# Two of the seven Strassen products split once more into 128x128 blocks, with the masks on GpSimd, the norm in one ScalarE operation and a new order of the steps

## The chip, the cores and the metric

The kernel runs on one core of a Trainium2 chip. The metric is the device time of one execution in microseconds (us), median of several. A ratio is the mean time of one kernel's fast runs over the mean of the fast runs of the kernel before in the same rounds, so it is not quite the ratio of the medians beside it. Spans and positions inside a group come from one profiled execution each; "wait" is the time by which TensorE's matmuls start further apart than their usual pitch, averaged over the 28 inner groups of four batches. In the profiles PE is TensorE's matmuls and PEld its weight loads, DVE VectorE, ACT ScalarE, POOL GpSimd and SPq the queue of SyncE, which issues DMAs.

## The reference, cut to what matters

```python
h = relu(layernorm(x))                                   # x: 128 batches x 128 nodes x 512
A = einsum('od,bdn->bon', adj, h); C = A + b             # same matrix twice, so (C - A) is the bias
x = x + max over nodes of relu(A + b)
h = relu(layernorm_of_the_new_x)
q, k, v = h @ Wq + bq, h @ Wk + bk, h @ Wv + bv          # 512 x 512, 8 heads of 64
w = softmax(q k^T / 8 + (-1e9 where adj == 0))
out = x + w v
```

The first layer adds one number to each row of x, which the layer norm of the second removes again. So the kernel norms x once. Nearly all arithmetic is in the three 512x512 projections, in f32.

## The kernel before: the parts that the argument touches

Batches go in groups of four. A projection of a group is a product of 512x512 by 512x512, done by Strassen's algorithm (Winograd's form) on 256x256 quarters: seven products P1 to P7 in place of eight. A product is eight matmul instructions of 256 columns (four f32 matmuls in two instructions each). VectorE (DVE) adds up the products, because each PSUM bank holds a running sum that several results share.

```python
class Products:                       # one projection ("q", "k" or "v") of a group; cut
    def p1(self):
        self.a = self.bank(0);  self.mm(self.a, "a11", "b11", True)
        ...                           # ScalarE copies bank a out, with two biases: p1a, p1b
    def p6(self):
        self.b = self.bank(1);  self.mm(self.b, "s2", "t2", True)
        nc.vector.tensor_tensor(self.u2, self.b, self.pf[0], op=ALU.add)
    def p2(self):
        self.mm(self.a, "a12", "b21");  self.biased(self.dst(0, 0), self.a, 0)
    def p7(self):
        self.mm(self.b, "s3", "t3")
        nc.vector.tensor_tensor(self.u3, self.b, self.pf[1], op=ALU.add)
    def p5(self):
        self.c = self.bank(2);  self.mm(self.c, "s1", "t1", True)
        self.add(self.dst(1, 1), self.c, self.u3)
    def p4(self):
        self.mm(self.b, "a22", "t4");  self.add(self.dst(1, 0), self.b, self.pf[1])
    def p3(self):
        self.mm(self.c, "s4", "b22");  self.add(self.dst(0, 1), self.c, self.u2)
...
part = (v.p1, v.p6, v.p2, v.p7, v.p5, v.p4, q.p1, v.p3, q.p6, q.p2, q.p7, q.p5,
        q.p4, k.p1, q.p3, k.p6, k.p2, k.p7, k.p5, k.p4, k.p3)      # TensorE's order in a group
```

Each group begins with `apply` (w v of the group before) and `scores` (q k^T), then come the projections. The masks multiply w by 0 where adj is 0. Between those steps stands the work for the group after next: `norm` (the layer norm), `adjacency` (the product with adj), `blocks` (a DVE transpose in 32x32 blocks) and `move`, which brings the blocks of a pair of batches into their places, 16 DMAs for each pair on SyncE's queue. `h_sum` makes the quarter sums t1 to t4 from what has landed.

## Time and profile before

| | |
|---|---|
| median | 1546.77 us (1546.75 to 1548.46) |
| period of a group, start of apply to start of apply | 47.55 us |
| first apply starts / last apply to the end | 88.9 / 13.0 us |
| waits in TensorE's stream, per group | about 0.5 us, all at the three changes of matmul kind (k to apply, apply to scores, scores to v); the same in the changed kernel |

The page says how busy each engine was, and the chain which work ended last; the prediction shows both.

The columns are start, duration, engine, line, operation and count.

### The profile page before, as it was taken

The numbers are of one execution on the slowest core, as the hardware profiler recorded it, in microseconds if no ns is written. First come the engines' busy times: TensorE is split into PE (matmuls) and PEld (weight loads), VectorE is DVE, ScalarE is ACT, GpSimd is POOL, SyncE is SP. The second block draws the span as 40 slices with busy tenths as digits, with TensorE's granted clock in tenths as the row PEclk, the third lists the DMA queues.
The fourth block names the chain that finished last, engine by engine and source line by source line (L and its number), as shares of the span: only waits on it lengthen the run. The fifth ranks groups of instructions, "written<-read, shape, count | busy, mean of one in ns | idle before, by whom it ended". The sixth has DMA issues, their size and how long they took to land.

```text
span 1544.7 us, 29809 instructions
## 1 busy us (share of the span) xinstructions
PE 1528.1 (99%) x11805; PEld 1310.5 (85%) x11805; DVE 1129.9 (73%) x2115; ACT 415.2 (27%) x844; POOL 272.4 (18%) x278
## 2 busy tenths in 40 slices
PE   7999999999999999999999999999999999999997
PEld 6888888888888888888888888888888888888886
DVE  7677777777777777777777777777777777777756
ACT  3322223222232222332222322223222133222221
POOL 5411122111221111220112211122111122011200
PEclk9999999999999999999999999999999999999999
DMA  5223322123221232222332212322123221233101
GB/s 180 35 72 80 78 59 72 49 75 83 56 74 48 72 83 55 78 49 71 80 75 60 72 49 76 83 55 74 49 72 83 55 77 47 72 80 74 36 30 56
DMA packets 307789, 105.10 MB, mean 68 GB/s; under 512 B 273152, under 2 KB 273280, under 8 KB 307648
## 3 DMA queue, kind: packets, MB, share of 16 engines
q1 hardware_dynamic: 306352, 101.00, 25.3%
q8 instruction: 95, 1.56, 0.4%
q10 hardware_dynamic: 1120, 1.90, 0.4%
q14 instruction: 46, 0.38, 0.1%
q0 software_dynamic: 176, 0.27, 0.1%
HBM read 37.03 MB, written 33.55 MB: 46 GB/s over the span
## 4 chain that ended last, share of the span: by engine, by line
PE 98%; DMA 1%; DVE 0%; ACTq 0%; ACT 0%; POOL 0%; DVEq 0%; issue 0%
PE bk L387 75%; PE bk L512 8%; PE bk L482 8%; PE bk L321 7%; PE bk L458 1%; DMA xg<-in_x_dram 1%; DVE o L530 0%; ACTq L237 0%; DVE o L540 0%; DVE live L552 0%; ACT hn L283 0%; POOL rstd L275 0%; DVE st L270 0%; PE bk L315 0%; DVE RS L529 0%; DVEq L668 0%
## 5 line engine op out<-in xcount | busy, mean ns | idle before, releaser
L275 POOL TENSOR_TENSOR rstd<-ve,mhalf 128x1 f32<-128x1 f32 x128 | 83.6, 653 | 1039.6 <-DVE ve L273 1023.5
L490 ACT ACTIVATE w<-bk 128x512 f32<-128x512 f32 x256 | 128.8, 625 | 401.6 <-PE bk L482 401.6
L289 POOL TENSOR_TENSOR xg<-xg,bv_sb 128x512 f32<-128x512 f32 x128 | 173.6, 1357 | 140.6 <-DVE hn L280 140.6
L494 DVE TENSOR_TENSOR w<-w,live 128x512 f32<-128x512 f32 x256 | 184.4, 731 | 0.4 <-ACT w L490 0.4
L387 PE MATMUL bk<-hs,sk_sb 128*128 128x256 f32 x768 | 181.1, 379 | 0.0
L387 PE MATMUL bk<-sv_sb,hs 128*128 128x256 f32 x768 | 176.2, 379 | 0.0
L387 PE MATMUL bk<-hs,sq_sb 128*128 128x256 f32 x744 | 175.6, 379 | 0.0
L387 PEld LDWEIGHTS bk<-hs,sk_sb 128*128 128x128 f32 x768 | 145.9, 190 | 33.5 <-issue 7.9
L283 ACT ACTIVATE hn<-hn,rstd 128x512 f32<-128x512 f32 x128 | 92.5, 723 | 283.8 <-DVE hn L280 257.0
L387 PEld LDWEIGHTS bk<-hs,sq_sb 128*128 128x128 f32 x744 | 141.4, 190 | 32.0 <-issue 7.2
L387 PEld LDWEIGHTS bk<-sv_sb,hs 128*128 128x128 f32 x768 | 145.9, 190 | 19.8
L426 DVE TENSOR_TENSOR u<-bk,p1a 128x512 f32<-128x512 f32 x95 | 65.7, 692 | 125.9 <-PE bk L387 125.9
L321 PE MATMUL bk<-hn,adjT 128*128 128x512 f32 x256 | 131.4, 596 | 0.0
L512 PEld LDWEIGHTS bk<-v,w 128*64 128x64 f32 x4096 | 122.1, 137 | 10.6 <-issue 10.6
L512 PE MATMUL bk<-v,w 128*64 128x65 f32 x4096 | 126.5, 222 | 0.0
L387 PE MATMUL bk<-wv_sb,hT 128*128 128x256 f32 x512 | 124.3, 386 | 0.0
L482 PE MATMUL bk<-qT,kT 64*128 64x128 f32 x2048 | 122.9, 275 | 0.0
L387 PE MATMUL bk<-hT,wk_sb 128*128 128x256 f32 x512 | 121.0, 379 | 0.0
L482 PEld LDWEIGHTS bk<-qT,kT 64*128 64x128 f32 x2048 | 116.8, 188 | 2.5 <-issue 0.3
L387 PE MATMUL bk<-hT,wq_sb 128*128 128x256 f32 x496 | 117.2, 379 | 0.0
L387 PEld LDWEIGHTS bk<-hT,wq_sb 128*128 128x128 f32 x496 | 94.2, 190 | 25.6 <-issue 14.3
L387 PEld LDWEIGHTS bk<-hT,wk_sb 128*128 128x128 f32 x512 | 97.3, 190 | 13.2
(87 smaller groups left out, 1994.8 us busy)
## 6 DMA issues: line engine op xcount, KB each, us to landing
out_dram<-o SPq DMA_DIRECT2D x128, 256.0 KB, 2.2
xg<-in_x_dram SPq DMA_DIRECT2D x62, 512.0 KB, 4.7
hT<-tb SPq DMA_DIRECT2D x992, 32.0 KB, 1.9
wq_sb<-in_L_gnn_Wq_dram SPq DMA_DIRECT2D x2, 512.0 KB, 6.8
xg<-in_x_dram ACTq DMA_DIRECT2D x3, 256.0 KB, 7.0
wk_sb<-in_L_gnn_Wk_dram SPq DMA_DIRECT2D x1, 512.0 KB, 11.2
wv_sb<-in_L_gnn_Wv_dram SPq DMA_DIRECT2D x1, 512.0 KB, 12.2
wk_sb<-in_L_gnn_Wk_dram ACTq DMA_DIRECT2D x1, 512.0 KB, 9.7
```

The lines of the kernel that those rows point to most:

```text
L275: nc.gpsimd.tensor_tensor(rstd, ve, mhalf, op=ALU.pow)
L283: nc.scalar.activation(HN[m], HN[m], AF.Copy, scale=RSTD[m])
L289: nc.gpsimd.tensor_tensor(x_m, x_m, bv_sb, op=ALU.add)
L321: nc.tensor.matmul(pa, adjT, HN[m], start=True, stop=True)
L387: nc.tensor.matmul(bank[:, r, :], lhs, rhs, start=first and r == 0 and c == 0, stop=r == 1 and c == 1, skip_group_check=True,)
L426: nc.vector.tensor_tensor(self.u2, self.b, self.pf[0], op=ALU.add)
L458: nc.tensor.matmul(pq[:, r, :], W["q"][:, c, (2 * f + r) * P : (2 * f + r + 1) * P], h[:, :, c], start=r == 0 and c == 0, stop=r == 1 and ...
L482: nc.tensor.matmul(psc[j][:, f, :], KT[g][r, f, i * D : (i + 1) * D], QT[g][r, f, i * D : (i + 1) * D], start=True, stop=True,)
L490: nc.scalar.activation(w[:, j], psc[j], AF.Exp, scale=HD ** -0.5)
L494: nc.vector.tensor_tensor(w[:, j], w[:, j], live_h, op=ALU.mult)
L512: nc.tensor.matmul(pav[r, c : c + HE], w[:, h % 2, h // 2, r], V[:, i, h, :], start=True, stop=True,)
```

## The change

It has three intents. P4 and P3 are split by the same algorithm into 128x128 blocks: seven block products M1 to M7 for each of the two, so 14 f32 matmuls of 128 columns in place of eight of 256. To give DVE room for the extra additions, the masks go to GpSimd and the norm becomes one ScalarE operation. And as the blocks need a scratch bank, the banks and the order of the whole group are dealt anew. The core of the diff, cut:

```diff
+            def p43(self):                 # in place of p4 and p3, both at once (k = 0, 1)
+                scr = bank(6).rearrange("p (m k d) -> p m k d", m=2, k=2)
+                def m1(k): mm(scr[:, 0, k], ...)      # M1, M6, M7 one after another in here
+                def m5(k): mm(scr[:, 1, k], ...)      # same bank, other half
+                ...
+                m1(0), m1(1), m5(0), m5(1)
+                more(u[:, :, 0, 0], scr[:, 0])        # DVE: u += M1
+                m2(0), m3(0), m6(0), m6(1)
+                more(u[:, :, 0, 1], scr[:, 0])
+                m4(0), m2(1), m3(1), m4(1), m7(0), m7(1)
+                ...                                   # four more additions of u
+                self.add(self.dst(1, 0), self.b, self.u[:, 0])
+                self.add(self.dst(0, 1), self.c, self.u[:, 1])
...
         def norm_end(m):
-            nc.vector.tensor_scalar(HN[m], X[g][:, i, :], MV[m][:, 0:1], 0.0, op0=ALU.subtract, op1=ALU.max)
-            nc.scalar.activation(HN[m], HN[m], AF.Copy, scale=RSTD[m])
+            nc.scalar.activation(HN[m], x_of(m), AF.Relu, scale=RSTD[m], bias=NMR[m])
...
-            pa = bank(5 + i % 2)
+            pa = bank(7)
...
-                6: [(blocks, m)], 7: [(blocks, m + 1), (move, m + 1)],
-                ...
-                14: [(blocks, m + 3), (move, m + 3)],
-                17: [(adjacency, m + 2)], 19: [(adjacency, m + 3)],
+                6: [(norm, m + 1)], 7: [(norm_end, m + 1)], 8: [(blocks, m), (adjacency, m)],
+                9: [(norm, m + 2)],
+                12: [(blocks, m + 1), (move, m + 1), (norm_end, m + 2), (adjacency, m + 1)],
+                13: [(norm, m + 3)], 14: [(norm_end, m + 3), (adjacency, m + 2), (blocks, m + 2)],
+                15: [(blocks, m + 3), (move, m + 3)], 16: [(adjacency, m + 3)],
...
+                for p in [Products(g, "v")] + [Products(g + 1, n) for n in "qk" if g + 1 < NG]:
+                    part += p.p1, p.p6, p.p2, p.p7, p.p5, p.p43
...
-                    for k, s in enumerate((6, 9, 12, 13, 15, 16, 17, 18)):
-                        add(s, mask, b + k // 2, k % 2)
+                    for k, s in enumerate((9, 10, 11, 12, 13, 14, 15, 16)):
+                        add(s, mask, nc.gpsimd, b + k // 2, k % 2)
```

So there are 18 steps to a group now, six for each projection; steps 6 to 11 are q's, 12 to 17 k's.

More of the change, by code (lines that the diff above doesn't have):

```diff
@@ L188, in tile_adj_preln_d2 @@
     WS = {n: const.tile([P, 4, 2, N // 2], F32, name=f"s{n}_sb") for n in "qkv"}
+    WB = {n: const.tile([P, 2, 4, P], F32, name=f"ss{n}_sb") for n in "qkv"}
     b0_sb = const.tile([P, 1], F32, name="b0_sb")
@@ L202, in fast @@
     def fast(ctx):
-        xpool = ctx.enter_context(tc.tile_pool(name="xpool", bufs=4))
+        xpool = ctx.enter_context(tc.tile_pool(name="xpool", bufs=7))
         proj = ctx.enter_context(tc.tile_pool(name="proj", bufs=2))
@@ L211, in fast, with x_of, load @@
         CNT, w_of, O = [], {}, {}
-        X, HN, TB, HT, HB, QT, KT, C, AMAX, WA, RSTD, MV, PR = ({} for _ in range(13))
+        X, HN, TB, HT, HB, H2, QT, KT, C, AMAX, WA, RSTD, NMR, PR = ({} for _ in range(14))
         def bank(k):
             return ps.tile([P, 512], F32, name=f"bk{k}")
-        def load(g):
-            X[g] = xpool.tile([P, G, N], F32, name="xg")
-            for i in range(0, G, 2):
-                nc.sync.dma_start(
-                    X[g][:, i : i + 2, :],
-                    x[g * G + i : g * G + i + 2].rearrange("b p n -> p b n"),
-                )
+        def x_of(b):
+            return X[b // 2][:, b % 2, :]
+        def load(p):
+            X[p] = xpool.tile([P, 2, N], F32, name="xp")
+            nc.sync.dma_start(X[p], x[2 * p : 2 * p + 2].rearrange("b p n -> p b n"))
         def load_w(eng, name, h):
@@ L234, in fast @@
         nc.scalar.dma_start(adj_sb, adj)
-        X[0] = xpool.tile([P, G, N], F32, name="xg")
+        for p in range(2):
+            X[p] = xpool.tile([P, 2, N], F32, name="xp")
         for i in range(G):
-            (nc.scalar if i > 0 else nc.sync).dma_start(X[0][:, i, :], x[i])
+            (nc.scalar if i > 0 else nc.sync).dma_start(x_of(i), x[i])
         load_w(nc.sync, "q", 0)
@@ L247, in fast @@
         nc.gpsimd.dma_start(bv_sb, bv.rearrange("(o f) -> o f", o=1).to_broadcast([P, N]))
-        load(1)
-        load(2)
+        for p in range(2, 5):
+            load(p)
         make_identity(nc, ident)
@@ L266, in norm @@
                 C[g] = stat.tile([P, G], F32, name="c")
-            HN[m] = work.tile([P, N], F32, name="hn")
+            HN[m] = work.tile([P, N], F32, name="hn", bufs=3)
             st = stat.tile([P, 6], F32, name="st")
             mv = stat.tile([P, 2], F32, name="mv")
-            nc.vector.bn_stats(st, X[g][:, i, :])
+            nc.vector.bn_stats(st, x_of(m))
             nc.vector.bn_aggr(mv, st)
@@ L275, in norm @@
             nc.gpsimd.tensor_tensor(rstd, ve, mhalf, op=ALU.pow)
-            MV[m] = mv
+            nmr = NMR[m] = stat.tile([P, 1], F32, name="nmr")
+            nc.gpsimd.tensor_scalar(nmr, mv[:, 0:1], rstd, -1.0, op0=ALU.mult, op1=ALU.mult)
         def norm_end(m):
-            g, i = divmod(m, G)
-            nc.vector.tensor_scalar(
-                HN[m], X[g][:, i, :], MV[m][:, 0:1], 0.0, op0=ALU.subtract, op1=ALU.max
-            )
-            nc.scalar.activation(HN[m], HN[m], AF.Copy, scale=RSTD[m])
+            nc.scalar.activation(HN[m], x_of(m), AF.Relu, scale=RSTD[m], bias=NMR[m])
             if m >= G:
@@ L287, in add_bv @@
         def add_bv(m):
-            x_m = X[m // G][:, m % G, :]
+            x_m = x_of(m)
             nc.gpsimd.tensor_tensor(x_m, x_m, bv_sb, op=ALU.add)
@@ L339, in h_sum, with h_blocks, weight_blocks @@
             nc.vector.tensor_sub(HB[g][o], HB[g][a], HB[g][b])
+        def h_blocks(g, k):
+            if k == 0:
+                H2[g] = one.tile([P, 2, 4, D], F32, name="h2")
+            b, t = HB[g]["t4 b22".split()[k]].rearrange("p t c d -> p c t d"), H2[g][:, k]
+            nc.vector.tensor_sub(t[:, 0:2], b[:, :, 1], b[:, 0])
+            nc.vector.tensor_sub(t[:, 2], b[:, 1, 1], t[:, 0])
+            nc.vector.tensor_sub(t[:, 3], b[:, 1, 0], t[:, 2])
+        def weight_blocks(eng, n):
+            for k in range(2):
+                a = WA[n]["a22 s4".split()[k]].rearrange("p c (o f) -> p o c f", o=2)
+                s = WB[n][:, k]
+                for o, x, op, y in (
+                    (s[:, 0], a[:, 1, 0], ALU.add, a[:, 1, 1]),
+                    (s[:, 2], s[:, 0], ALU.subtract, a[:, 0, 0]),
+                    (s[:, 1], a[:, 0, 0], ALU.subtract, a[:, 1, 0]),
+                    (s[:, 3], a[:, 0, 1], ALU.subtract, s[:, 2]),
+                ):
+                    eng.tensor_tensor(o, x, y, op=op)
         def weight_sum(eng, n, k):
@@ L363, in __init__ @@
                 self.g, self.n = g, n
+                self.k0 = 3 if n == "q" else 0
                 if n == "q":
@@ L393, in bank @@
             def bank(self, k):
-                return bank(k).rearrange("p (r n) -> p r n", r=2)
+                return bank(self.k0 + k).rearrange("p (r n) -> p r n", r=2)
             def biased(self, out, bank, f):
@@ L412, in p1 @@
                 self.mm(self.a, "a11", "b11", True)
-                self.pf = [tmp.tile([P, 2, HT2], F32, name="p1a")]
+                self.u = tmp.tile([P, 2, 2, HT2], F32, name="u")
                 if self.n == "v":
+                    self.pf = [self.u[:, 0]] * 2
                     nc.scalar.copy(self.pf[0], self.a)
-                    self.pf.append(self.pf[0])
                 else:
-                    self.pf.append(tmp.tile([P, 2, HT2], F32, name="p1b"))
+                    self.pf = [tmp.tile([P, 2, HT2], F32, name="p1a", bufs=1), self.u[:, 0]]
                     for f in range(2):
@@ L424, in p6 @@
                 self.mm(self.b, "s2", "t2", True)
-                self.u2 = tmp.tile([P, 2, HT2], F32, name="u2")
-                nc.vector.tensor_tensor(self.u2, self.b, self.pf[0], op=ALU.add)
+                nc.vector.tensor_tensor(self.u[:, 1], self.b, self.pf[0], op=ALU.add)
             def p2(self):
@@ L440, in p5, with blk, mm, m1 @@
                 self.add(self.dst(1, 1), self.c, self.u3)
+            def p43(self):
+                a = [WA[self.n][k].rearrange("p c (o f) -> p o c f", o=2) for k in ("a22", "s4")]
+                b = [HB[self.g][k].rearrange("p t c d -> p c t d") for k in ("t4", "b22")]
+                s, t = WB[self.n], H2[self.g]
+                scr = bank(6).rearrange("p (m k d) -> p m k d", m=2, k=2)
+                def blk(x):
+                    if self.n == "v":
+                        return x.rearrange("p t (o d) -> p o t d", o=2)
+                    return x.rearrange("p o (t d) -> p o t d", t=2)
+                def mm(out, w, h, start=False):
+                    lhs, rhs = (h, w) if self.n == "v" else (w, h)
+                    nc.tensor.matmul(
+                        out, lhs, rhs, start=start, stop=True, skip_group_check=True
+                    )
+                bc = [blk(self.b), blk(self.c)]
+                u = self.u.rearrange(
+                    "p k t (o d) -> p k o t d" if self.n == "v" else "p k o (t d) -> p k o t d",
+                    d=D,
+                )
+                def m1(k):
+                    mm(scr[:, 0, k], a[k][:, 0, 0], b[k][:, 0, 0], start=k == 0)
+                def m2(k):
+                    mm(bc[k][:, 0, 0], a[k][:, 0, 1], b[k][:, 1, 0])
+                def m3(k):
+                    mm(bc[k][:, 0, 1], s[:, k, 3], b[k][:, 1, 1])
+                def m4(k):
+                    mm(bc[k][:, 1, 0], a[k][:, 1, 1], t[:, k, 3])
+                def m5(k):
+                    mm(scr[:, 1, k], s[:, k, 0], t[:, k, 0])
+                def m6(k):
+                    mm(scr[:, 0, k], s[:, k, 2], t[:, k, 2])
+                def m7(k):
+                    mm(scr[:, 0, k], s[:, k, 1], t[:, k, 1])
+                def more(to, what):
+                    nc.vector.tensor_tensor(to, to, what, op=ALU.add)
+                m1(0), m1(1), m5(0), m5(1)
[3 more added lines that the diff above has]
+                m4(0), m2(1), m3(1), m4(1), m7(0), m7(1)
+                for o in range(2):
+                    more(u[:, :, o, 1], scr[:, 1])
+                for t_ in range(2):
+                    more(u[:, :, 1, t_], scr[:, 0])
+                self.add(self.dst(1, 0), self.b, self.u[:, 0])
+                self.add(self.dst(0, 1), self.c, self.u[:, 1])
@@ L447, in p3 @@
                 self.mm(self.c, "s4", "b22")
-                self.add(self.dst(0, 1), self.c, self.u2)
+                self.add(self.dst(0, 1), self.c, self.u[:, 1])
         def plain_q(t, f):
@@ L490, in scores, with mask @@
                     nc.scalar.activation(w[:, j], psc[j], AF.Exp, scale=HD ** -0.5)
-        def mask(b, j):
+        def mask(eng, b, j):
             w = w_of[b]
-            nc.vector.tensor_tensor(w[:, j], w[:, j], live_h, op=ALU.mult)
+            eng.tensor_tensor(w[:, j], w[:, j], live_h, op=ALU.mult)
         def apply(g, n_last=G):
@@ L537, in residual @@
             y = O[g][:, i]
-            x_b, c_b = X[g][:, i, :], C[g][:, i : i + 1]
+            x_b, c_b = x_of(b), C[g][:, i : i + 1]
             if eng is nc.vector:
@@ L559, in next_norms @@
             return {
-                1: [(norm, m)], 2: [(norm_end, m), (norm, m + 1)], 4: [(norm_end, m + 1)],
-                6: [(blocks, m)], 7: [(blocks, m + 1), (move, m + 1)],
-                8: [(adjacency, m)], 9: [(norm, m + 2)],
-                10: [(adjacency, m + 1), (norm_end, m + 2)],
-                11: [(norm, m + 3)], 12: [(norm_end, m + 3)], 13: [(blocks, m + 2)],
-                14: [(blocks, m + 3), (move, m + 3)],
-                17: [(adjacency, m + 2)], 19: [(adjacency, m + 3)],
+                1: [(norm, m)], 2: [(norm_end, m)],
+                6: [(norm, m + 1)], 7: [(norm_end, m + 1)], 8: [(blocks, m), (adjacency, m)],
[3 more added lines that the diff above has]
+                15: [(blocks, m + 3), (move, m + 3)], 16: [(adjacency, m + 3)],
             }
@@ L575, in fast @@
                     transposes(m - 1)
+                if m == 2:
+                    adjacency(0)
             nc.vector.tensor_single_scalar(live, adjT, 0.0, op=ALU.not_equal)
-            for m in (2, 3):
-                adjacency(m - 2)
-                transposes(m)
+            transposes(2)
+            adjacency(1)
+            transposes(3)
             adjacency(2)
@@ L607, in fast @@
                     f(m)
+            weight_blocks(nc.gpsimd, "v")
             weight_sums(nc.gpsimd, "q")
+            weight_blocks(nc.gpsimd, "q")
             for m in range(G):
                 add_bv(m)
+            weight_blocks(nc.gpsimd, "k")
             for g in range(NG):
@@ L615, in fast @@
                 scores(g)
-                v = Products(g, "v")
-                if g + 1 < NG:
-                    q, k = [Products(g + 1, n) for n in "qk"]
-                    part = (
-                        v.p1, v.p6, v.p2, v.p7, v.p5, v.p4, q.p1, v.p3, q.p6, q.p2, q.p7, q.p5,
-                        q.p4, k.p1, q.p3, k.p6, k.p2, k.p7, k.p5, k.p4, k.p3,
-                    )
-                else:
-                    part = (v.p1, v.p6, v.p2, v.p7, v.p5, v.p4, v.p3)
+                part = []
+                for p in [Products(g, "v")] + [Products(g + 1, n) for n in "qk" if g + 1 < NG]:
+                    part += p.p1, p.p6, p.p2, p.p7, p.p5, p.p43
                 todo = {s: [] for s in range(len(part))}
@@ L628, in add @@
                     todo[s].append(what)
+                if g == 0:
+                    for k in range(2):
+                        h_blocks(0, k)
                 if g + 1 < NG:
@@ L633, in fast @@
                             residual(b - G + i)
-                    for k in range(4):
-                        add((0, 3, 5, 8)[k] if g > 0 or k == 3 else 3 + k, h_sum, g + 1, k)
+                    for k, s in enumerate((0 if g else 3, 2 if g else 3, 3, 7)):
+                        add(s, h_sum, g + 1, k)
+                    for k, s in enumerate((8, 9)):
+                        add(s, h_blocks, g + 1, k)
                     if g + 2 < NG:
@@ L640, in fast @@
                     else:
-                        add(4, count, 0, b)
-                    for k, s in enumerate((6, 9, 12, 13, 15, 16, 17, 18)):
-                        add(s, mask, b + k // 2, k % 2)
+                        add(6, count, 0, b)
+                    for k, s in enumerate((9, 10, 11, 12, 13, 14, 15, 16)):
+                        add(s, mask, nc.gpsimd, b + k // 2, k % 2)
+                    if g + 2 < NG:
+                        add(0, load, 2 * g + 5)
                     if g + 3 < NG:
-                        add(10, load, g + 3)
+                        add(8, load, 2 * g + 6)
                 else:
-                    for k, s in enumerate((0, 0, 0, 1, 2, 2, 3, 4)):
-                        add(s, mask, b + k // 2, k % 2)
-                    for i, s in enumerate((0, 1, 2, 3)):
+                    for k, s in enumerate((0, 0, 0, 1, 2, 2, 3, 3)):
+                        add(s, mask, nc.vector, b + k // 2, k % 2)
+                    for i, s in enumerate((0, 1, 2, 5)):
                         add(s, residual, b - G + i)
```

## The prediction

> **What bounds the kernel now.** I read the page first, then the chain of waits in order of time, then the timeline of one group of four batches.
>
> ```profile
> PE 1528.1 (99%) x11805; PEld 1310.5 (85%) x11805; DVE 1129.9 (73%) x2115; ACT 415.2 (27%) x844; POOL 272.4 (18%) x278
> ...
> PE 98%; DMA 1%; DVE 0%; ACTq 0%; ACT 0%; POOL 0%; DVEq 0%; issue 0%
> PE bk L387 75%; PE bk L512 8%; PE bk L482 8%; PE bk L321 7%; PE bk L458 1%; DMA xg<-in_x_dram 1%; DVE o L530 0%; ACTq L237 0%; DVE o L540 0%; DVE live L552 0%; ACT hn L283 0%; POOL rstd L275 0%; DVE st L270 0%; PE bk L315 0%; DVE RS L529 0%; DVEq L668 0%
> ```
>
> The chain is TensorE alone, three quarters of it in the projections (L387). It waits for nobody: DVE has 27% spare, ACT and POOL far more. In the merged chain,
>
> ```profile
> 96.57 15.74 PE bk L387 x72
> 117.48 12.09 PE bk L387 x56
> 144.12 15.74 PE bk L387 x72
> ```
>
> 12.09/56 = 0.216 us per matmul instruction of 256 columns (each f32 matmul is two instructions), and 144.12 - 96.57 = 47.55 us is the period of a group. It adds up without a hole: 84 products' matmuls x 2 x 0.216 = 36.3, adjacency 3.4, scores 3.8, apply 3.9. So anything that shortens TensorE's stream pays at once, and any wait put into that stream costs at once.
>
> **What the Trainium skill says.**
> - "TensorE: Matmul & The Clock Gate", Back-to-back issue gap: N/2.4 + 2.5 ns. With two passes, 512/2.4 + 2.5 = 216 ns: the trace agrees. For 128 columns this gives 109 ns.
> - Same page, LDWEIGHTS: columns/1.2, so 107 ns for 128 columns. The trace's loads take 190 ns for 128 columns and 138 for 64, a slope of 0.81 ns per column: agrees. A 128-column matmul is thus just as long as the load that it must hide.
> - "PSUM — Partial Sum Buffer", PSUM bank collisions raise a hardware error: no two engines may touch one bank at a time, disjoint columns included. The kernel before keeps readers and writers in different banks; the changed kernel's scratch bank does not, see below.
> - "SBUF — State Buffer", Who interferes with whom: a DVE tensor_tensor with two SBUF inputs contends with GpSimd's reads. The trace agrees: the same weight sums take 1214 to 1749 ns on DVE beside GpSimd's, against 692 for such an operation alone.
>
> The 128-column rate itself is seen in the transposes (full 128x128 loads):
>
> ```profile
> 12.77 0.72 ACT L283 ACTIVATE hn<-hn,rstd 128x512 f32<-128x512 f32 x1 [0.91 <-POOL rstd L275]
> ...
> 13.54 0.42 PEld L315 LDWEIGHTS bk<-ident,hn 128*128 128x128 f32 x4 [1.25 <-ACT hn L283]
> 13.55 0.65 PE L315 MATMUL bk<-ident,hn 128*128 128x128 f32 x4 [0.43 <-ACT hn L283]
> ```
>
> A single one lasts 272 ns; four take 0.65, of which the first is late, the rest 109 apart. Two other numbers come from here: ACT ends at 13.49 and the load starts at 13.54, so a release costs TensorE 0.05; and after a wait the first load is exposed. At the switch to the scores, whose loads are of the ordinary kind, the gap is 0.21 instead of 0.105: 0.105 us per wait.
>
> **The change part by part.** Per group, three projections replace 2 x 4 matmuls of 256 columns (16 x 0.216 = 3.46 us) by 14 of 128 (28 x 0.110 = 3.08): gain 0.38 each, 1.13 us a group. There are 94 such pairs (32 v, 31 q, 31 k): 35 us, 2.3%, is all that can be won.
>
> DVE: six additions of 256 columns per pair (425 ns by form, a pitch of 0.34; L530 128x256) = 2.0 us, so 6 us more a group, and 1.9 for the h blocks; away go eight masks (5.8) and four first halves of the norm (1.9). The sum changes by +2 of 35 us: not a bound. POOL gets 8 masks x 1.3 us and four small operations: about 22 of 47 us. ACT: one pass of the norm as before. None of these busy sums matters; the order does.
>
> 1. *Scratch bank.* Of the 14 matmuls, M1, M1, M5, M5 go to one bank, DVE reads M1, then M2, M3 run elsewhere, then M6 writes the bank again. In the built program DVE's read waits for the second M5, not M1 (same bank), and M6 waits for the read. From the end of M5's stream: last matmul done +0.16 (272 - 109), DVE starts +0.04, 0.425 reading, release 0.05, exposed load 0.105 = 0.78. M2 and M3 cover only 4 x 0.109 = 0.44. Wait 0.34 us, with an idle DVE. M7, behind four matmuls (0.87), does not wait. The start delay is read here:
>
> ```profile
> 797.64 1.89 PE L387 MATMUL bk<-hs,wk_sb 128*128 128x256 f32 x8
> ...
> 799.57 0.69 DVE L408 TENSOR_TENSOR kT<-bk,p1b 128x512 f32<-128x512 f32 x1 [0.44 <-PE bk L387]
> ```
>
> 2. *q: DVE's queue.* In the built order there stand, between q's P7 addition and its P5 addition, three h-block subtractions, each dependent on the one before (0.45 + 0.32 + 0.20), and a whole norm:
>
> ```profile
> 779.88 0.68 DVE L270 BATCH_NORM_STATS2 st<-xg 128x6 f32<-128x512 f32 x1
> 780.59 0.18 DVE L271 BATCH_NORM_AGGREGATE mv<-st 128x2 f32<-128x6 f32 x1
> 780.88 0.15 DVE L273 TENSOR_SCALAR ve<-mv 128x1 f32<-128x1 f32 x1
> 780.95 0.68 DVE L494 TENSOR_TENSOR w<-w,live 128x512 f32<-128x512 f32 x1
> ```
>
> 780.95 - 779.88 = 1.07. Start after P7's end 0.27, + 0.61 + 0.97 + 1.07 = 2.92; P5's addition 0.61; M1's reading 0.425; release and load 0.155: M6 at 4.11 after P7, where TensorE alone would be there at 1.73 + 1.31 = 3.04. Wait 1.07 in q (in place of 0.34). In v and k DVE is free in time.
>
> 3. *q's P2.* It writes the bank that ACT reads four times (p1a, p1b):
>
> ```profile
> 774.61 0.84 ACT L402 ACTIVATE p1a<-bk,bq_sb 128x256 f32<-128x256 f32 x2 [1.61 <-PE bk L387]
> 775.33 0.84 ACT L402 ACTIVATE p1b<-bk,bq_sb 128x256 f32<-128x256 f32 x2
> ```
>
> ACT is done at 776.17, 1.83 after P1's stream ended (774.34). Before, P1 and P2 of q had two products between them; now only P6 (1.73). Wait 0.10 + 0.05 + 0.105 = 0.26. In k an adjacency matmul lies between: none.
>
> 4. *The block transposes' DMAs.* A pair of batches is moved by 16 DMAs on one queue:
>
> ```profile
> 777.64 10.39 SPq L306 DMA_DIRECT2D hT<-tb  x16
> ...
> 791.41 10.40 SPq L306 DMA_DIRECT2D hT<-tb  x16
> ```
>
> With the group's start at 754.4, the second ended at time 47.4, and its first reader (L339) comes at 8 of the next group: free. In the changed order the first move follows q's whole block, which with the added waits puts it at 37.5; the second queues behind it, 48 to 58 or 60, and lands 1.9 later, which is 11.3 to 13.3 of the next group. DVE's first h sum, in front of v's P6 addition, sits there. P7 needs that addition: landing + 0.6 + 0.7 + 0.15, against TensorE's 13.1. Wait 0 to 1.6, say 0.65.
>
> 5. *Scores.* k's last additions now take DVE 3 us instead of 0.7 before it can empty the apply banks; the bank of the eighth heads comes free about when the last scores want it: 0.1 to 0.2.
>
> Sum per group: 2 x 0.34 + 1.07 + 0.26 + 0.65 + 0.15 = 2.81 of waits against 1.13 of gain: +1.68, over 31 groups +52, and 2 for the end, where masks stay on DVE and the last additions lengthen the tail: 1601. I shade it to 1592, since these kernels come tuned and some wait may be shorter than the built order suggests.
>
> **Rivals.**
> (a) TensorE's stream stays closed, and the gain comes through: 1510 to 1515. For it: DVE has slack and the order M1, M5, M2, M3, M6 looks made for cover. Against: the wait on the second M5 is in the built program, and the latencies are from the trace.
> (b) Only the local waits (1, 2, 3) count, DMAs stay in time: waits 2.0 against 1.13, +27 us, 1575: "same" by the 2% rule. Its only question is step 4.
> (c) Loads do not hide behind 128 columns: at 0.190 a matmul, a pair costs 5.3 instead of 3.1 and the kernel goes to about 1720 to 1750. Against: the transposes' 109 (though their loads last 140 to 190 ns, the ordinary ones 190) and the scores' pitch of 0.112 per row group with the same loads.
> (d) GpSimd becomes late with the masks and apply waits for them. It would end its last mask at about the start of apply; those are read 2.9 us later. With contention at 1.65 us a mask this is nearly eaten up. Worth up to 1 us a group.
>
> **Range and chances.** Waits 1 to 3 are worked out from measured latencies and I trust them to a third; 4 and 5 can be nothing or twice as much. Low end 1555: half of 2 and none of 4. High end 1625: 4 in full. Faster by 2% needs nearly no wait at all: 0.05. Within 2% (to 1578) needs steps 4 and 5 absent: 0.27. Slower: 0.68.
>
> **What would show it.** TensorE's share of the chain falls below 95%, with DVE and perhaps DMA in it; matmuls of the block products with idle time before them "<-DVE u", longest in q; ACT before q's P2; the period of a group at 48.5 to 50 us; the 128-column matmuls at 109 to 112 ns where they do not wait; DVE's first h sum waiting for the hT DMA. I am wrong if TensorE's busy share stays at 99% (then a), or if block matmuls lie near 190 ns apart (c).

## More of the kernel before

One more line belongs to the argument: SyncE's view around one group's start.

```profile
777.64 10.39 SPq L306 DMA_DIRECT2D hT<-tb  x16
788.13 2.06 SPq L221 DMA_DIRECT2D xg<-in_x_dram  x2
791.41 10.40 SPq L306 DMA_DIRECT2D hT<-tb  x16
```

## The result, and the profile after

The changed kernel takes **1646.1 us** (1645.7 to 1647.37, 4 runs) against 1546.76 for the kernel before in the same rounds: ratio 1.064 (95% interval 1.0622 to 1.0659). It is right in its results, and 99 us slower, where the prediction had 45 and a range up to 1625.

First come the engines' busy times and the chain of waits, from the page of the changed kernel:

```profile
PE 1545.2 (94%) x12933; PEld 1330.8 (81%) x12933; DVE 1170.9 (71%) x2495; ACT 423.2 (26%) x844; POOL 621.2 (38%) x678
...
PE 52%; SPq 25%; DVE 14%; issue 4%; DMA 4%; DVEq 0%; ACT 0%; ACTq 0%; POOL 0%
PE bk L414 33%; SPq L309 25%; PE bk L484 11%; PE bk L324 5%; DVE u L516 3%; DMA hT<-tb 3%; DVE qT L435 2%; DVE u L453 1%; DVE u L462 1%; PE bk L600 1%; DVE st L276 1%; PE bk L570 1%; DVE amax L325 1%; PE bk L546 1%; DMA xp<-in_x_dram 1%
```

TensorE has fallen from 98% of the chain to 52%. A quarter now belongs to SyncE's queue at L309, which is `move`; in the kernel before that queue isn't in the chain at all. DVE's own share of busy time has hardly changed (73% to 71%): it has not become the bound by volume.

The view of waits names who waited for whom (us in total, times, longest):

```profile
DVE hs L342 <- DMA hT<-tb: 109.0, 29, 5.4
PEld bk L414 <- DVE u L453: 54.1, 31, 3.2
PEld bk L484 <- DVE u L516: 53.2, 94, 2.1
PE bk L414 <- DVE u L453: 41.9, 30, 2.8
PE bk L484 <- DVE u L516: 33.1, 62, 1.9
```

Read it from the top as a chain. DVE's h sum (L342) waits 3.8 us in each of 29 groups for a transfer. Behind that sum, in DVE's queue, stands the addition after P6 (L453), and TensorE waits for it with P7. The other pair is the scratch bank (L484 are the block matmuls, L516 the additions of u). The loads (PEld) and the matmuls (PE) tell of the same waits twice, so they aren't added.

One group shows the first of these in order of time. From the chain of waits:

```profile
800.88 3.88 PE bk L600 x128
804.77 3.80 PE bk L570 x64
808.56 5.39 PE bk L414 x24
813.95 0.03 issue
813.98 0.70 DVE u L453
814.68 0.04 issue
814.72 3.72 PE bk L414 x16
818.44 0.91 PE bk L484 x8
819.35 0.02 issue
819.37 0.43 DVE u L516
819.80 0.04 issue
819.85 2.05 PE bk L484 x16
```

Apply, scores, P1, P6 and P2 run without a hole up to 813.95. Then 0.77 us of DVE stand in the chain before P7 starts at 814.72; this is one of the shorter waits, the mean is 1.70. At 819.35 the last M5 is out of the array; DVE reads M1 for 0.43 us, and M6 may start only at 819.85. M2 and M3 run meanwhile and cover a part of it, and 0.34 us of wait are left. Why DVE was late with L453 is in SyncE's view of the same moment:

```profile
789.49 22.29 SPq L309 DMA_DIRECT2D hT<-tb  x32
811.88 2.01 SPq L632 DMA_DIRECT2D out_dram<-o  x4
```

The two pairs' 32 DMAs have become one unbroken run, from 11.4 us before the group's start (800.88) to 10.9 after it. It cannot land in time for an h sum wanted at 8.

Here is where the 100.9 us of the profiled span (1544.7 to 1645.6) went:

| | before | after | share |
|---|---|---|---|
| first apply starts | 88.85 | 95.25 | +6.4 |
| 29 periods | 47.55 each | 50.50 mean (49.28 to 53.39) | +85.7 |
| last two periods, shorter in work | 44.11 + 19.94 | 46.71 + 20.09 | +2.8 |
| last apply to the end | 12.96 | 18.99 | +6.0 |

### The profile page after: what moved, and what is told of

Same layout as the page of the kernel before. It is cut to its first block, busy times and chain, and to the rows that moved or that the text cites. A ratio compares the mean times of both kernels' runs of the same rounds, so it can differ in the third digit from the quotient of the medians.

```text
span 1645.6 us, 32909 instructions
## 1 busy us (share of the span) xinstructions
PE 1545.2 (94%) x12933; PEld 1330.8 (81%) x12933; DVE 1170.9 (71%) x2495; ACT 423.2 (26%) x844; POOL 621.2 (38%) x678
## 4 chain that ended last, share of the span: by engine, by line
PE 52%; SPq 25%; DVE 14%; issue 4%; DMA 4%; DVEq 0%; ACT 0%; ACTq 0%; POOL 0%
PE bk L414 33%; SPq L309 25%; PE bk L484 11%; PE bk L324 5%; DVE u L516 3%; DMA hT<-tb 3%; DVE qT L435 2%; DVE u L453 1%; DVE u L462 1%; PE bk L600 1%; DVE st L276 1%; PE bk L570 1%; DVE amax L325 1%; PE bk L546 1%; DMA xp<-in_x_dram 1%
## 5 line engine op out<-in xcount | busy, mean ns | idle before, releaser
L516 DVE TENSOR_TENSOR u<-u,bk 128x256 f32<-128x256 f32 x564 | 211.3, 416 | 168.3 <-PE bk L484 168.1
L582 POOL TENSOR_TENSOR w<-w,live 128x512 f32<-128x512 f32 x248 | 312.2, 1280 | 6.9 <-ACT w L578 6.9
L414 PE MATMUL bk<-sv_sb,hs 128*128 128x256 f32 x768 | 184.3, 391 | 41.9 <-DVE u L453 41.9
L292 POOL TENSOR_TENSOR xp<-xp,bv_sb 128x512 f32<-128x512 f32 x128 | 162.4, 1270 | 133.8 <-ACT hn L286 133.8
L414 PE MATMUL bk<-hs,sk_sb 128*128 128x256 f32 x768 | 176.2, 379 | 0.0
L414 PE MATMUL bk<-hs,sq_sb 128*128 128x256 f32 x744 | 170.8, 379 | 0.0
L286 ACT ACTIVATE hn<-xp,nmr,rstd 128x512 f32<-128x512 f32 x128 | 104.5, 817 | 190.4 <-POOL nmr L283 190.4
L342 DVE TENSOR_TENSOR hs<-hT 128x512 f32<-128x512 f32 x64 | 47.6, 744 | 113.7 <-DMA hT<-tb 109.0
L414 PE MATMUL bk<-hT,wq_sb 128*128 128x256 f32 x496 | 120.5, 386 | 0.0
L325 DVE TENSOR_REDUCE amax<-bk 128x1 f32<-128x512 f32 x128 | 86.0, 672 | 35.5 <-PE bk L324 35.5
## 6 DMA issues: line engine op xcount, KB each, us to landing
wv_sb<-in_L_gnn_Wv_dram SPq DMA_DIRECT2D x1, 512.0 KB, 12.4
wk_sb<-in_L_gnn_Wk_dram ACTq DMA_DIRECT2D x1, 512.0 KB, 10.4
```

The costliest lines, as they stand in the source:

```text
L286: nc.scalar.activation(HN[m], x_of(m), AF.Relu, scale=RSTD[m], bias=NMR[m])
L292: nc.gpsimd.tensor_tensor(x_m, x_m, bv_sb, op=ALU.add)
L325: nc.vector.reduce_max(AMAX[g][:, i : i + 1], pa, axis=AX.X)
L414: nc.tensor.matmul(bank[:, r, :], lhs, rhs, start=first and r == 0 and c == 0, stop=r == 1 and c == 1, skip_group_check=True,)
L516: nc.vector.tensor_tensor(to, to, what, op=ALU.add)
L582: eng.tensor_tensor(w[:, j], w[:, j], live_h, op=ALU.mult)
```

## The experiments

The theory after reading the trace: the block products save what they should (about 1 us a group), but their waits take four times that, and the largest is the late move. The main rival: it is the rest of the change (masks and norm on other engines, the new order), not the blocks and what hangs on them.

### 1. The side parts alone on the kernel before

```diff
 # kernel before, plus:
-            nc.vector.tensor_scalar(HN[m], X[g][:, i, :], MV[m][:, 0:1], 0.0, op0=ALU.subtract, op1=ALU.max)
-            nc.scalar.activation(HN[m], HN[m], AF.Copy, scale=RSTD[m])
+            nc.scalar.activation(HN[m], X[g][:, i, :], AF.Relu, scale=RSTD[m], bias=MV[m])   # MV = -mean*rstd
-                        add(s, mask, b + k // 2, k % 2)
+                        add(s, mask, nc.gpsimd, b + k // 2, k % 2)
```

> The kernel before with only the two side parts: masks of all groups but the last on GpSimd, the norm as one Relu on ScalarE with scale and bias. Theory of the waits (the loss is TensorE waiting for DVE and the DMAs around the block products): nothing of this is on TensorE's chain, 1547 us, 1543 to 1551, TensorE 99% busy. Rival (GpSimd beside DVE slows the shared port, or the longer norm chain is late): 1580 us or more.

Measured: 1548.03 us, ratio 1.001 (0.9993 to 1.0026), as expected.

```profile
PE 1529.6 (99%) x11805; PEld 1310.8 (85%) x11805; DVE 969.8 (63%) x1739; ACT 427.2 (28%) x844; POOL 616.2 (40%) x654
...
PE 97%; DVE 2%; DMA 0%; issue 0%; ACT 0%; POOL 0%; DVEq 0%; ACTq 0%; POOLq 0%
```

DVE loses 160 us of work and GpSimd gains 344; nothing comes of either, since TensorE still is the chain. The period is 47.55 as before. The side parts by themselves are neither gain nor loss.

### 2. The new order without the block products

```diff
 # changed kernel:
-                    part += p.p1, p.p6, p.p2, p.p7, p.p5, p.p43
+                    part += p.p1, p.p6, p.p2, p.p7, p.p5, lambda p=p: (p.p4(), p.p3())
```

> The changed kernel with its whole schedule, but the last two products of each projection whole again (no blocks, no scratch bank, no six additions). Theory of the waits: the waits at M6 vanish, q's P2 keeps its 0.2 us, and as DVE reaches the block transposes 2 us earlier the DMAs land just in time, 0 to 0.3 us a group: 1562 us, 1553 to 1570. Rival (the new order, with the late transposes' DMAs, costs the same without the blocks): 1600 us or more.

Measured: 1574.99 us, ratio 1.0183 (1.0166 to 1.02): between the two, 13 us over the theory's figure and 25 under the rival's. The period is 48.15, which is 47.55 plus two waits: 0.20 for ScalarE before q's P2, and 0.40 in q, where P3 waits for DVE's late addition after P5. Over 29 periods that is 17 of the 27 us by which the profiled span is longer. The rest is at the ends: the first apply is 5 us later, the tail 3 longer, the last two periods 1. From the view of waits:

```profile
DVE hs L342 <- DMA hT<-tb: 82.5, 29, 3.5
PEld bk L414 <- DVE qT L435: 15.4, 29, 0.5
PEld bk L414 <- DVE u L453: 1.4, 4, 0.8
```

DVE's first h sum waits for the move here as well, 2.8 us each time, but P7 hardly ever waits (1.4 us in all). So the late move alone is harmless: in the changed kernel it needed the delay that the block products bring to be late enough. New order: +28 us. Blocks on top of it: +71, where TensorE's shorter stream alone would have given about -31.

### 3. The first pair's move four steps earlier

```diff
-                6: [(norm, m + 1)], 7: [(norm_end, m + 1)], 8: [(blocks, m), (adjacency, m)],
+                6: [(norm, m + 1)], 7: [(norm_end, m + 1)],
+                8: [(blocks, m), (blocks, m + 1), (move, m + 1), (adjacency, m)],
-                12: [(blocks, m + 1), (move, m + 1), (norm_end, m + 2), (adjacency, m + 1)],
+                12: [(norm_end, m + 2), (adjacency, m + 1)],
```

> The changed kernel with the first pair's block transposes and its 16 DMAs four products earlier (after q's P2, before q's block product); nothing else. Theory of the waits: the wait of v's P7 (1.70 us a group in the trace) and the slowed clock after it go, the four waits at M6 and q's P2 stay: 31 x 1.8 = 56 us less, 1590 us, 1582 to 1600. Rival (the DMA wait only hides other waits behind it, DVE being late anyway): 1625 us or more.

Measured: 1592.12 us, ratio 1.0291 (1.0274 to 1.0308), as expected. SyncE's view again shows two runs with a pause:

```profile
756.50 10.40 SPq L309 DMA_DIRECT2D hT<-tb  x16
767.00 0.55 SPq L229 DMA_DIRECT2D xp<-in_x_dram  x1
772.83 11.05 SPq L309 DMA_DIRECT2D hT<-tb  x16
```

and in the view of waits the 109.0 us have become

```profile
DVE hs L342 <- DMA hT<-tb: 0.6, 1, 0.6
```

The wait before P7 is gone from every inner group, the other waits stay (v 0.34, q 0.98, k 0.52, q's P2 0.20), and the period is 48.61. This shows the cause by taking it away: the late move cost 1.9 us a group, 54 us in all.

### 4. In addition, the norm out of q's DVE queue

```diff
 # experiment 3, plus:
-                9: [(norm, m + 2)],
+                11: [(norm, m + 2)],
```

> As the run with the early move, and the norm of batch 2 moved out of the queue in front of q's P5 addition to behind q's block product. Theory of the waits: q's wait at M6 falls from 1.06 to about 0.34 us, 31 x 0.72 = 22 us less than the early move alone, 1568 us, 1560 to 1578; if that norm then comes late for its adjacency matmul, up to 10 us of it are lost. Rival (the wait at M6 in q comes from the bank or the h blocks, not from the norm): no gain over the early move.

Measured: 1614.01 us, ratio 1.0438 (1.042 to 1.0455). This is a plain miss: 46 us over the expectation, and slower than without the edit. The norm did leave DVE's queue, yet q's M6 waits 0.92 where it waited 0.98, and k's 0.99 in place of 0.52. The late norm costs something too, as the expectation had allowed for: TensorE waits 0.21 for its adjacency matmul in k. The timeline of q in one group says why:

```profile
811.18 1.27 POOL L292 TENSOR_TENSOR xp<-xp,bv_sb 128x512 f32<-128x512 f32 x1 [0.93 <-ACT hn L286]
...
812.41 2.49 POOL L582 TENSOR_TENSOR w<-w,live 128x512 f32<-128x512 f32 x2
...
813.67 1.52 DVE L350 TENSOR_TENSOR h<-hT 128x256 f32<-128x256 f32 x1
```

The small power of the norm on GpSimd had held back the masks behind it in that queue until DVE was through with its h blocks. Without it the masks run earlier, and the h block (L350) takes 1.52 us beside a mask in place of 0.41. It is the contention of which the prediction spoke, two SBUF inputs on DVE beside GpSimd's reads, and here is its size. What looked like a wait that could be taken away was also a spacer.

### 5. The scratch in two banks

```diff
-                scr = bank(6).rearrange("p (m k d) -> p m k d", m=2, k=2)
+                scr = [bank(j).rearrange("p (m k d) -> p m k d", m=2, k=2)[:, 0]
+                       for j in (6, 2 if self.n == "q" else 5)]       # M1, M6, M7 / M5
```

> The changed kernel with M5's scratch in a second bank (a bank of the other projection's set, free at that time), so that DVE's read of M1 waits for M1 and not for M5; nothing else. Theory of the waits: only v gains, its wait at M6 goes from 0.34 to about 0.08 us; in q and k DVE's queue arrives later than the bank would allow, so they stay at 1.06 and 0.51: 8 us less, 1638 us, 1633 to 1643. Rival (the shared bank is what costs at M6 in all three): 31 x 3 x 0.34 = 32 us less, 1614 us.

Measured: 1611.74 us, ratio 1.0418 (1.0391 to 1.0445). v's M6 waits 0.04 in place of 0.34, and q and k stay where they were (1.04, 0.51), as said. The total, however, is 26 us better than the theory's figure and close to the rival's; the single waits tell where that is from: the wait before P7 halved as well, from 1.70 to 0.86. In the trace the first move starts 12.0 us before the group's start instead of 11.3, and the h sum at 12.4 instead of 13.2. The traces show why: with M5 in a bank of its own, DVE begins to read it 0.57 us before q's last block matmul starts, in place of 0.31 after it. DVE's last addition of u then ends 0.67 sooner, and the block transposes and the move follow 0.67 sooner as well. What the prediction had taken from the rule on banks (the page has it for each quarter of a bank's partitions; the tiles here span them all) holds in v, where DVE is free: M6 waits with one bank and not with two. That a collision raises an error is something no run here shows.

### 6. Experiment 4 with the masks elsewhere

```diff
-                    for k, s in enumerate((9, 10, 11, 12, 13, 14, 15, 16)):
+                    for k, s in enumerate((4, 4, 5, 5, 12, 13, 14, 15)):
                         add(s, mask, nc.gpsimd, b + k // 2, k % 2)
```

> As the run with the early move and the late norm, but with GpSimd's masks away from the h blocks: four of them during v's products and four after the late norm. In that run the h block's first subtraction took 1520 instead of 412 ns beside a mask, and the C operation 906 instead of 230. Theory (that norm had held GpSimd's masks back; with it gone they ran into DVE's operations with two SBUF inputs): q's wait at M6 falls to about 0.34, k's to about 0.5: 1575 us, 1566 to 1586. Rival (the late norm itself costs it): no better than 1614.

Measured: 1589.2 us, ratio 1.0273 (1.0256 to 1.029), 3 us outside the expected range. q's M6 waits 0.34, which is the scratch bank alone, as expected: with norm and mask both out of the way, q's extra wait is gone, so the reason given in experiment 4 holds. But k's M6 waits 0.93. From DVE's and GpSimd's timelines at the end of k:

```profile
818.89 0.71 DVE L299 STREAM_TRANSPOSE tb<-hn 128x512 f32<-128x512 f32 x1 [0.65 <-ACT hn L286]
819.52 0.65 DVE L435 TENSOR_TENSOR kT<-bk,u 128x512 f32<-128x512 f32 x1
820.13 0.69 DVE L325 TENSOR_REDUCE amax<-bk 128x1 f32<-128x512 f32 x1
820.85 0.86 DVE L327 TENSOR_SCALAR c<-amax,b_sb 128x4 f32<-128x4 f32 x1
821.63 0.41 DVE L516 TENSOR_TENSOR u<-u,bk 128x256 f32<-128x256 f32 x1
```

```profile
817.96 1.28 POOL L582 TENSOR_TENSOR w<-w,live 128x512 f32<-128x512 f32 x1
819.19 1.27 POOL L292 TENSOR_TENSOR xp<-xp,bv_sb 128x512 f32<-128x512 f32 x1
820.43 2.49 POOL L582 TENSOR_TENSOR w<-w,live 128x512 f32<-128x512 f32 x2
```

DVE first waits 0.65 for a norm that was late through GpSimd's queue. Then L327, four columns of arithmetic, takes 0.86 us beside a mask; in the kernel before its median is 0.23. Ahead of the first block addition (L516), that is what TensorE waits for.

### 7. All the waits at once

```diff
 # experiments 5 and 6 together, plus:
-                8: [(blocks, m), (blocks, m + 1), (move, m + 1), (adjacency, m)],
+                7: [..., (adjacency, m)],  8: [(blocks, m), (blocks, m + 1), (move, m + 1)],
-            if i == G - 1:  nc.vector.tensor_scalar(C[g], ...)        # L327: inside the adjacency
+                17: [(c_of, m // G)]                                   # now behind k's block product
-                    for i, s in enumerate((0, 1, 2, 5)):  add(s, residual, ...)
+                    for i, s in enumerate((0, 1, 2, 3)):  add(s, residual, ...)
+                    # v of the last group: whole p4, p3; adjacency of the first two groups in banks 5, 6
```

> All mended: early move, late norm, masks away, two scratch banks, q's adjacency between P6 and P2, C after the last block product, the first adjacencies in two banks, the last group's v without blocks. If the list of waits is complete, 0.3 us of waits a group are left against 1.16 of gain, a period of 46.8 us: 1524 us, 1515 to 1538, faster than both kernels. If block products cost something that is not in the list, 1547 or more.

Measured: 1542.85 us, ratio 0.9975 (0.9958 to 0.9991). It is the first version that is faster than the kernel before, if by a quarter of a per cent; the expectation was 1524 (1515 to 1538), so that is a miss. The period is 47.13, the tail 12.85 as before. Left over are 0.50 us in q and a start that is 7 us late. The wait in q is this pair, from one group's timeline:

```profile
780.53 1.27 POOL L292 TENSOR_TENSOR xp<-xp,bv_sb 128x512 f32<-128x512 f32 x1 [0.93 <-ACT hn L286]
780.79 1.29 DVE L353 TENSOR_TENSOR h<-hs 128x256 f32<-128x256 f32 x1
```

The h block (now L353) takes 1.29 us beside the addition of v's bias.

### 8. The masks back on DVE

```diff
 # changed kernel:
-                        add(s, mask, nc.gpsimd, b + k // 2, k % 2)
+                        add(s, mask, nc.vector, b + k // 2, k % 2)
```

> The changed kernel with the masks back on DVE at the same places in the order. Theory of the waits: they stand in front of M1's and M6's reads and of the late transposes, 1 to 2.5 us a group more: 1680 us or more, 1670 to 1730. Rival (masks on GpSimd cost more by the shared port than they save on DVE): 1646 or less.

Measured: 1707.66 us, ratio 1.1042 (1.1024 to 1.1061), as expected. q's M6 waits 2.27 and k's 1.62. So moving the masks was worth 62 us to the changed kernel, though worth nothing by itself in experiment 1.

### 9. The bias elsewhere, and the start in the old order

```diff
 # experiment 7, plus:
-            if m >= G:  add_bv(m)
+            if m >= G and (m < 2 * G or m % G != 1):  add_bv(m)
-                11: [(norm, m + 2)],
+                11: [(norm, m + 2), (add_bv, m + 1)],
+            # v of the first group: whole p4, p3; its weight blocks are made last; start as in the kernel before
```

> The mended version once more, with three things its own trace showed. (1) In q the scratch bank still waits 0.40 + 0.10 us a group: DVE's first h-block subtraction takes 1290 ns instead of 410 because GpSimd adds the bias of v to x at the same moment; that addition is moved behind the third norm's operations on GpSimd. (2) The start goes back to the order of the kernel before (adjacency behind the transposes): first q product 1.2 us earlier. (3) The first v has whole P4 and P3, so that GpSimd makes q's weight blocks first: the waits of 2.1 and 1.65 us in the first group go. If contention makes the wait in q: period 47.13 -> 46.6 us, start 5 us shorter, in all 1522 us (1517 to 1530), 1.5% below the kernel before. Rival: the q wait is only the length of DVE's queue (transposes and additions), contention or not; then the period stays at 47.0 to 47.2 and only the start gains: 1535 to 1538. If the mask that now runs later collides with k's last additions, the k wait comes back (0.3 or more) and the sum ends between the two.

Measured: 1529.16 us, ratio **0.9883** (0.9866 to 0.9899): 1.2% faster than the kernel before, at the upper end of the range.

```profile
PE 1507.3 (99%) x12909; PEld 1329.5 (87%) x12909; DVE 1168.0 (76%) x2477; ACT 430.2 (28%) x844; POOL 623.4 (41%) x678
...
PE 94%; POOL 2%; DVE 2%; DMA 1%; issue 0%; ACT 0%; ACTq 0%; DVEq 0%; POOLq 0%
```

```profile
774.98 0.41 DVE L353 TENSOR_TENSOR h<-hs 128x256 f32<-128x256 f32 x1
```

The h block is back to 0.41 us, the wait in q fell from 0.50 to 0.04, and the period is 46.68. The part about the start failed: the first apply is at 96.40 (95.88 in experiment 7), because the waits in the first v were exchanged for one of 2.4 us in the first q's blocks. About 7 us more are to be had there; this was not tried.

## Why the prediction was wrong in size

The mechanism was right, and so was the direction: TensorE's stream was closed, every new wait counted in full, and there were more of them than gain. Its steps, per group in us (the last row for the whole run):

| term of the sum | predicted | measured |
|---|---|---|
| gain of the shorter stream | 1.13 | 1.0 |
| 1, scratch bank, v | 0.34 | 0.34 |
| 1, scratch bank, k | 0.34 | **0.51** |
| 2, DVE's queue in q | 1.07 | 1.06 |
| 3, ScalarE before q's P2 | 0.26 | 0.20 |
| 4, late move, before P7 | 0.65 | **1.70**, and 0.16 for a slower clock after it |
| 5, scores | 0.15 | 0 |
| net per group | +1.68 | +2.95 |
| outside the groups, in all | 2 | **15** |

*The step that failed* is the fourth: the move was foreseen as late, with a wait "0 to 1.6, say 0.65", and it was the size that was off. The prediction put the h sum at 11.3 to 13.3 of the group and took about the middle; the trace has it at 13.2 on average, near the late end. With the slower clock after it the wait is 1.21 us above the prediction's, which over 29 periods is 35 of the 54 us that were missed; the ends are 13 and the shading 9. The late end was the right one to take for a further reason: the landing is now set by a queue that never pauses. The prediction took all 32 issues at the pace of the quoted runs (16 in 10.4 us, 0.65 each, nothing slow among them). In the changed kernel two of 32 took 0.93 to 2.15 us, mean 1.48 (63 of 992; before 23 of 992, mean 1.35), and the 32 lasted 22.8 us where 20.8 had been counted. In the kernel before such an issue fell into a pause. The missing pause isn't what makes issues slow: experiments 3, 7 and 9, which have the pause, show 48, 60 and 57 slow ones of 992, and experiment 2, without the block products, 57. With the side parts alone there are 23, so the further ones came with the new order. Experiment 3 shows the whole term: with the first move earlier and the pause back, P7 doesn't wait and 54 us return. It doesn't part the late start of the move from its slow issues.

The long waits brought something that wasn't in the prediction at all. In three of the 28 groups TensorE then ran at half its pace for a while, 3.41 us each time by the trace's record of the clock. From the windows of such a group (window, length, then busy time of PE, PEld, DVE, ACT and POOL, the granted clock, DMA share, GB/s):

```profile
1355.40:1366.00 10.60, 10.60 (x207) 10.07 (x207) 8.90 (x20) 4.61 (x9) 0.00 (x0) 1.00 0.29 49
1366.00:1372.00 6.00, 3.74 (x17) 3.00 (x16) 2.46 (x6) 0.59 (x1) 0.15 (x1) 0.98 0.75 246
1372.00:1380.00 8.00, 7.93 (x43) 6.84 (x43) 4.52 (x8) 0.81 (x1) 2.30 (x3) 0.80 0.26 92
```

The wait falls into the second window; in the third PE is busy throughout, at 0.80 of its clock. Eight of the matmuls there are 0.427 us apart instead of 0.216. The Trainium skill has this on "TensorE: Matmul & The Clock Gate", Part 1: The HAM clock gate: an idle window halves the array's clock until it has been busy for one. The trace agrees in kind, halved pace included; the last section has the length of the wait.

*Step 1 in k* was predicted like v, with "an idle DVE". DVE wasn't idle: L327 stood in front of the block addition and took 0.44 us beside a GpSimd mask (the chain shows it at 847.73) instead of 0.23. Rival (d) had looked for GpSimd's contention in apply only. Experiments 4, 6, 7 and 9 show that it matters, and where. The prediction's own range for it, 1214 to 1749 ns, mixed two cases: 1214 is the mean of one weight sum that took 679 and one that took 1750; those beside GpSimd took 1640 to 1750.

*Step 5* did not come: scores start without an extra wait.

*The ends* were set at 2 us and took 15. The last residual was put behind the last block product, and apply's DVE write then waited for its store:

```profile
1630.03 0.11 DVE RS L617
1630.14 3.95 DMA out_dram<-o
1634.09 0.03 issue
```

That is 4 of the 6 us of the tail; experiment 7, with that residual two steps earlier and whole products in the last v, has the old tail. The start's 6.4 us stay open in part: two attempts moved the waits there without removing them.

*The rivals.* (a) fell, the stream didn't stay closed. (c) fell: block matmuls are 0.111 to 0.112 us apart where nothing holds them, against the 0.19 that it feared. (The section from which the prediction took its 109 ns gives the formula for an isolated matmul and says that it is too short for a stream with loads at 128 columns; the prediction left that out. The measured 0.1117 is under 3 ns above it.) (b), only the local waits, is what experiment 3 measures, in effect: 1592 where (b) said 1575, most of the difference being the ends. That experiment 3 meets the predicted time is chance; the move isn't late there. Shading the sum of 1601 down to 1592, for the reason that "these kernels come tuned", had no number behind it and went the wrong way. Of the signs named in advance, TensorE's share of the chain below 95%, waits on u with the longest of the block waits in q, ScalarE before q's P2, block matmuls at 0.111 to 0.112 and the h sum behind the DMA all came; the period came at 50.50, just over the 48.5 to 50 that were named.

## What to carry to other kernels

When one engine is the whole chain, a change that shortens its stream by 1 us a period may bring 4 us of waits with it, as here. Five of the six waits could be worked out beforehand to within 0.2 us from the built order and measured durations; the one that came out as a range, because it hung on a queue without pauses, came at its late end. Before moving work off a busy engine, ask what that work was spacing apart: an operation taken away (experiment 4) or moved to GpSimd (experiments 4, 6, 7) can land beside another that it slows, and one DVE operation of 0.4 us becomes 1.3 to 1.5. The change itself was sound: with its waits mended one by one from the trace, the same arithmetic is 1.2% faster than the kernel before instead of 6.4% slower.

## What the Trainium skill lacked or had wrong

- "TensorE: Matmul & The Clock Gate", Part 1: The HAM clock gate: the table of states has the clock halved after at least one idle window of about 3.4 us. Here it was halved after gaps of 2.25 to 3.4 us between two matmul starts (three groups of the changed kernel, at 2.64, 2.82 and 3.21 us), while other gaps of 2.70 and 2.73 us left it whole; with the masks on DVE several gaps of 2.25 us were enough, and the slow stretch begins up to 1.4 us after the gap. The 3.4 is from experiment 5.
- The same page's Back-to-back issue gap gives the gap of one instruction by its columns, without f32. Here an f32 matmul is two instructions, and each has about the gap of twice its columns: 0.216 us for 256 columns, 0.1117 for 128 (109 ns by the formula).
- No page has the price of one wait in a closed TensorE stream: 0.05 us from the other engine's end to the load, and 0.10 us of load exposed. It is in every wait above.
- "SBUF — State Buffer", Who interferes with whom, has the contention right: it calls the shared port pair "an exclusive lock", from which a size can be worked out, but has no durations for shapes like these. A DVE operation of 0.41 us took 1.29 to 1.52 us beside a GpSimd one of 1.27 and ended 0.28 us after it, in all 62 cases of experiments 4 and 7. A tensor_scalar of 128x4 took 0.43 to 0.91 us instead of 0.23 and ended 0.02 to 0.03 us after the GpSimd operation beside it, in all 96 cases of the changed kernel and experiments 4 and 6.
- "DMA: Bandwidth & Descriptors" gives 512 sequencer cycles for one DMA instruction of "previous generations", in a table on a later chip, and no time for SyncE's issue of a small strided SBUF-to-SBUF DMA here: 0.61 us for 32 KB, with a slow one of 0.9 to 2.15 us now and then, 23 of 992 in the kernel before and 63 of 992 in the changed one. Why they are slow no run here shows.
